# A deformable convolution and a mixture of experts on one core: the weight tables of the next image, with ten tent buffers across both halves of the partitions

## The chip, the cores and the metric

The kernel runs on one NeuronCore of a Trainium2 chip. The metric is the device time of one execution in microseconds (us); smaller is better. The core has five engines that each work through their own instructions in order: TensorE (PE, with its weight loads as PEld), VectorE (DVE), ScalarE (ACT), GpSimd (POOL) and SyncE (SP). SP, ACT and POOL also issue DMA transfers, each on its own queue.

## What is computed

The input is x, 8 images of 128 channels and 64 x 64 pixels, in f32. Two layers follow each other, each on a group-normalised input and with a residual:

```python
x = x + relu(batchnorm(deform_conv(gn(x))))       # layer 0
x = x + moe_conv(gn(x))                           # layer 1

# deform_conv, k = 3, for each image
om   = conv3x3(x, off_w) + off_b                  # 27 planes: 9 x (dy, dx), 9 masks
mask = sigmoid(om[:, 18:])
py, px = pixel + tap - 1 + (dy, dx)               # real-valued positions
val  = bilinear(x, py, px) * mask                 # zero outside the image
out  = einsum('bckhw,ock->bohw', val, w)
```

Layer 1 mixes four expert convolutions by a gate on the image's mean and adds a shared one. Batch normalisation needs the statistics of all 8 images, so layer 1 starts when layer 0 is over.

## The kernel before

`dense()` computes layer 0 without gathers. An offset smaller than 2 reaches 5 rows and 5 columns around each tap, so bilinear interpolation is a sum over these with weights max(0, 1 - |distance|), a "tent" in y and one in x. Tents are made for each of `NR = 5` distances. The y tents are multiplied by the mask.

**Bands.** An image is `NB = 8` bands of 8 rows. For a band, `pick` (L606) copies overlapping 8 x 8 pixel patches on DVE, `pixels` transposes them on PE (L621) and ACT copies them out of PSUM (L626) into `xt`. `weights` (L648, DVE) multiplies an x weight tile (`xwts`, three buffers) and a y weight tile (`ywts`, two buffers) to a matrix `s`. `sample` multiplies `xt` by `s` on PE (L664), ACT copies the result to `samples` (L674), and DVE copies an edge column of the first and last of the five groups (L686, L688). `conv` runs the nine taps of the deformable convolution on PE (L716); ACT adds the bias (L724), DVE takes statistics (L725), and SP stores the band (L726, `yd`).

**Tables.** The weight tiles come from two tables in DRAM for each image, `taby` and `tabx` (two copies, in turn). `load_x` (L592) and `load_y` (L577) bring a band's part in, issued on POOL two bands ahead: 2 loads of 576 KB and 8 of 90 KB. The generator `tables(b)` makes an image's tables while the image before is worked on:

- SP loads the image into `pads`; DVE takes statistics (L267); two small matmuls (L273, L283) and POOL (L289) give the group normalisation; ACT and DVE apply it (L295, L296).
- `combine` (L322, DVE) forms half sums of rows in two buffers, `combos`, and `tap` (L339, PE) runs the offset convolution on them; ACT and DVE collect it in `om` (L361, L368 to L383). ACT copies part of it with rows and columns exchanged (L388).
- SP stores it to DRAM as `rowwise` (L394) and `colwise` (L398) and loads it back spread over 64 partitions (L416, `spread`, 15 loads), as `off_y`, `mask` and `off_x` side by side on partitions 0 to 63 of `combos[1]`. DVE mends the edges (L441 to L444) and ACT takes the sigmoid of the mask (L448).
- For each of five distances: ACT makes the x tent (L505 the distance, L511 the tent), DVE the y tent (L516, L518) and its product with the mask (L524). SP stores both to the tables: `store_x` (L495, five or six transfers of up to 34 KB) and `store_y` (L468).

For images 1 to 7 the tents have two buffers of each kind, all on partitions 0 to 63:

```python
work = a1.tile([W, 2, 2, YSTEP], F32, name="work", tag="om")
tents = [[work[:, a, i % 2] for i in range(NR)] for a in range(2)]
```

**Order.** The schedule is by hand (`manual_schedule`): each engine runs its instructions in program order. The generator yields between its pieces (`pause`), and the band loop calls `next(made)` a fixed number of times: once after each of five sample groups, and once or twice after each convolution tap:

```python
for _ in range(1 if calls > TAPS else 1 + (done % 3 > 0)):
    next(made, None)
```

At band 6 of an image, what is left of the generator is run at once, and that for the image after the next starts.

**Head.** For image 0 the tables are made with nothing beside them. `FIRST = 3` bands' x tents are made and stored first (`early_x`), x stores alternating between POOL and SP, y stores on SP; then come the loads of bands 0 and 1, the x tents of the other columns, and their 28 stores on SP. `tabx` is laid out by patch row q, then row tile, then column: `QROW = NROW * XROW`.

`layer1()` follows; the change doesn't touch it.

Of the kernel before, what the change touches and what calls it, by code (L numbers as in the profile page):

```python
# [55 lines left out]
GROW = NR * YSTEP  # L56
XROW = (NCOL + 1) * T * XSTEP
QROW = NROW * XROW
# [5 lines left out]
def deform_moe_conv(  # L64
# [83 lines left out]
    def padded(pool, name):  # L148
# [12 lines left out]
        for a, n in (("y", (H + 2 * REACH) * GROW), ("x", Q * QROW))  # L161
# [15 lines left out]
    def dense():  # L177

        with ExitStack() as st:
# [32 lines left out]
            for i, at in ((0, 0), (1, H - 1)):  # L212
                nc.gpsimd.affine_select(
                    out=nudge[:, i : i + 1], in_=nudge[:, i : i + 1], compare_op=ALU.is_equal,
                    fill=0.0, base=-at, pattern=[[0, 1]], channel_multiplier=1,
                )

            combos = [a1.tile([P, H // 2, W], F32, name=f"combo{i}") for i in range(2)]
            flat = combos[1].rearrange("p h w -> p (h w)")
            three = flat[0:W, 0 : 3 * ROW].rearrange("p (t v k) -> p t v k", t=3, v=3)  # L220
            off_y, mask, off_x = (
                flat[0:W, i * ROW : (i + 1) * ROW].rearrange("p (v u j) -> p v u j", u=3, v=3)
                for i in range(3)
            )
            every_u = flat[0:W, 0 : 3 * ROW].rearrange("p (a u j) -> p a u j", u=3, j=WB)
            tent_y = combos[0].rearrange("p h w -> p (h w)")[0:W, 0:YSTEP]
# [16 lines left out]
            def tables(b):  # L243
# [8 lines left out]
                beside = nc.sync if b else nc.gpsimd  # L252
# [18 lines left out]
                yield from pause(3)  # L271
                pm = ps_c.tile([P, CH], F32, name="pm", tag="pc")
                nc.tensor.matmul(pm[:, 0:1], lhsT=gsel, rhs=mv[:, 0:1], start=True, stop=True)  # L273
                yield from pause(3)
# [6 lines left out]
                yield from pause(2)  # L281
                pv = ps_c.tile([P, CH], F32, name="pv", tag="pc")
                nc.tensor.matmul(pv[:, 0:1], lhsT=gsel, rhs=ev, start=True, stop=True)  # L283
                yield from pause(3)
                ve = small.tile([P, 1], F32, name="ve")
                nc.vector.tensor_scalar(ve, pv[:, 0:1], GN_EPS, None, ALU.add)
                yield from pause(2)
                scale = small.tile([P, 1], F32, name="scale")
                nc.gpsimd.tensor_tensor(scale, ve, nhalf, ALU.pow)  # L289
                yield from pause(3)  # L290
# [3 lines left out]
                for c in range(0, NCH, 2):  # L294
# [4 lines left out]
                    yield  # L299
# [10 lines left out]
                def combine(j):  # L310
# [5 lines left out]
                    for half in range(2):  # L316
# [5 lines left out]
                        nc.vector.tensor_tensor(  # L322
                            combo_of[j][:, half * n : half * n + n], *rows, op
                        )
                        yield
# [67 lines left out]
                for j in range(4):  # L393
# [4 lines left out]
                    beside.dma_start(  # L398
# [6 lines left out]
                if b == 0:  # L405
                    for g in range(2):
                        pick(g)
                    for _ in pixels(0):
                        pass
                yield from pause(9)  # L410
# [15 lines left out]
                for k in range(3):  # L426
# [6 lines left out]
                    for outs, parts, v in places:  # L433
                        for t, c in ((off_y, 3 * k), (mask, 2 * TAPS + 3 * k)):
                            spread(t, parts, v, nc.sync, by_row[outs, c : c + 3])
                        spread(
                            off_x, parts, v, nc.sync if b else nc.scalar,
                            colwise[b][k::3].rearrange("s w h -> w s h")[outs],
                        )
                yield from pause(14)  # L440
                nc.vector.tensor_copy(every_u[:, :, 0, 1:2], every_u[:, :, 2, 0:1])  # L441
                nc.vector.tensor_copy(every_u[:, :, 2, W : W + 1], every_u[:, :, 0, W + 1 : WB])
                for i in range(2):
                    nc.vector.tensor_scalar(  # L444
                        three[:, 0::2, 2 * i], three[:, 0::2, 2 * i], nudge[0:W, i : i + 1],
                        None, ALU.add,
                    )
                nc.scalar.activation(mask, mask, AF.Sigmoid)  # L448

                if b:  # L450
                    work = a1.tile([W, 2, 2, YSTEP], F32, name="work", tag="om")
                    tents = [[work[:, a, i % 2] for i in range(NR)] for a in range(2)]
                else:
                    one = samples[0].rearrange("p m x w -> p (m x w)")[0:W]
                    tents = [[one[:, i * YSTEP : (i + 1) * YSTEP] for i in range(NR)]]
                    one = combos[0].rearrange("p h w -> p (h w)")[0:W, YSTEP:]
                    n = FIRST * 2 * XSTEP
                    early_x = [one[:, i * n : (i + 1) * n] for i in range(NR)]
                    late = [om.rearrange("p a n -> p (a n)")[0:W], one[:, NR * n :]]
                    n = YSTEP - n  # L460
                    late_x = [late[i // 4][:, i % 4 * n : (i % 4 + 1) * n] for i in range(NR)]
# [922 lines left out]
```

## Time and profile before

| | us |
|---|---|
| median of 3 runs | 1786.99 (1786.05 to 1791.42) |
| the profiled execution | 1793.52 |
| its span | 1791.8 |
| PE busy | 1450.2 (81%) |
| DVE busy | 932.7 (52%) |
| ACT busy | 718.2 (40%) |
| POOL busy | 496.6 (28%) |
| first sample matmul (L664) starts | 89.33 |
| first band handed to ACT (L724) | 136.1 |
| last band handed to ACT | 1406.6 |

The span lies within the execution; 1.7 us are around it. The first 89 us are the head, then bands run to 1407, then layer 1. A share of busy time is an average over these: from 1461 on, in layer 1, PE is busy 322.4 of 330.8 us; from 127.7 to 1402 it is 1064.6 of 1274.3. "Granted clock" is the share of full speed that PE's clock had in a stretch. A wait names the instruction that was idle and what ended it; it costs time only where the idle engine holds up the one that sets the pace.

### The profile page before, as it was taken

Reading aid. Unit: us, or ns where it says so; the run is one execution under the profiler, and the core shown is the slowest. Engines: PE = TensorE matmul, PEld = TensorE weight load, DVE = VectorE, ACT = ScalarE, POOL = GpSimd, SP = SyncE. Lnnn points to the kernel's source line nnn. Section 1 sums busy time; section 2 is a strip of 40 time slices with the busy share of each in tenths; the row PEclk is TensorE's granted clock in tenths of the full one; section 3 lists DMA queues with packets and bytes.
Section 4 is the critical chain, followed back from the end, with each engine's and each line's share of the span. In section 5 each row is a group of like instructions: output and inputs, shape, how many; then the busy total and the mean of one; then the engine's idle time right before and its main releaser. Section 6 shows DMA issues by size and latency. Waiting matters only on the chain. (4 is left out here: it accounts for less than half of the span.)

```text
span 1791.8 us, 21276 instructions
## 1 busy us (share of the span) xinstructions
PE 1450.2 (81%) x7714; PEld 793.3 (44%) x7714; DVE 932.7 (52%) x1892; ACT 718.2 (40%) x984; POOL 496.6 (28%) x777
## 2 busy tenths in 40 slices
PE   4059758959986996899489869976999479999998
PEld 1045435426543653465255436543655234444443
DVE  5336435344633554364345345543333488888882
ACT  2224443445444543444354445344444323333330
POOL 2323123213321422232132224222332322232210
PEclk8569978979987998799789979987999789999999
DMA  5445456538454745555475547464664523334311
GB/s 184 109 96 134 102 132 147 129 78 202 105 129 109 192 109 129 138 144 135 86 179 127 125 100 193 119 140 94 167 168 113 198 92 141 141 150 152 132 48 61
DMA packets 169024, 234.31 MB, mean 131 GB/s; under 512 B 120026, under 2 KB 123384, under 8 KB 160460
## 3 DMA queue, kind: packets, MB, share of 16 engines
q0 software_dynamic: 59680, 122.86, 29.3%
q1 hardware_dynamic: 108432, 109.46, 20.4%
q8 instruction: 63, 1.03, 0.3%
q10 hardware_dynamic: 796, 0.52, 0.1%
q14 instruction: 53, 0.43, 0.1%
HBM read 180.23 MB, written 52.32 MB: 130 GB/s over the span
## 5 line engine op out<-in xcount | busy, mean ns | idle before, releaser
L716 PE MATMUL py<-samples,dw_sb 128*128 128x512 f32 (+3 forms) x1296 | 630.6, 600 | 101.0 <-ACT y L724 101.0
L577 POOL DMA_DIRECT2D ywts<-taby x508 | 303.9, 619 | 774.9 <-DVE s L648 706.4
L664 PE MATMUL pq<-s,xt 64*128 64x144 f32 (+1 forms) x3840 | 318.9, 309 | 60.8 <-DVE s L648 47.3
L674 ACT COPY samples<-pq 128x864 f32<-128x864 f32 (+1 forms) x320 | 296.7, 961 | 176.9 <-PE pq L664 176.8
L716 PEld LDWEIGHTS py<-samples,dw_sb 128*128 128x128 f32 x1296 | 225.4, 199 | 265.9 <-issue 127.9
L664 PEld LDWEIGHTS pq<-s,xt 64*128 64x128 f32 x3840 | 265.1, 192 | 171.0 <-issue 66.7
L626 ACT COPY xt<-pt 128x512 f32<-128x512 f32 (+1 forms) x256 | 142.8, 558 | 265.8 <-PE pt L621 264.8
L648 DVE TENSOR_TENSOR s<-xwts,ywts 128x432 f32<-128x432 f32 (+1 forms) x448 | 205.4, 495 | 84.3 <-PE pq L664 33.0
L621 PE MATMUL pt<-ident,picked 128*128 128x128 f32 x960 | 158.3, 287 | 96.9 <-ACT xt L626 92.9
L621 PEld LDWEIGHTS pt<-ident,picked 128*128 128x128 f32 x960 | 127.0, 148 | 236.5 <-issue 124.5
L1298 PE MATMUL pc<-v,u 128*128 128x512 f32 x384 | 172.8, 599 | 9.3 <-DVE u L1247 9.3
L1298 PE MATMUL pc<-v,wmix 128*128 128x512 f32 x384 | 176.3, 604 | 0.0
L688 DVE COPY samples<-pq 128x24 f32<-128x24 f32 x64 | 12.9, 201 | 278.5 <-ACT samples L674 278.5
L725 DVE BATCH_NORM_STATS2 ystats<-y 128x6 f32<-128x512 f32 (+3 forms) x72 | 45.7, 635 | 201.9 <-ACT y L724 201.9
L1298 PEld LDWEIGHTS pc<-v,u 128*128 128x128 f32 x384 | 72.4, 190 | 98.3 <-issue 85.8
L1298 PEld LDWEIGHTS pc<-v,wmix 128*128 128x128 f32 x384 | 72.6, 192 | 88.9 <-issue 85.2
L505 ACT ACTIVATE work<-combo,steps 64x576 f32<-64x576 f32 x35 | 46.3, 1323 | 146.6 <-DMA tabx<-work 120.3
L592 POOL DMA_DIRECT2D xwts<-tabx x128 | 75.1, 603 | 101.1 <-DMA tabx<-work 45.0
L1276 ACT ACTIVATE t<-pc,bmix 128x512 f32<-128x512 f32 x32 | 22.0, 687 | 183.1 <-PE pc L1298 101.1
L724 ACT ACTIVATE y<-py,db_sb 128x512 f32<-128x512 f32 (+3 forms) x72 | 45.7, 635 | 108.4 <-PE py L716 108.4
L322 DVE TENSOR_TENSOR combo<-pad 128x1024 f32<-128x1024 f32 x64 | 76.4, 1218 | 11.8 <-PE pc L339 9.9
L606 DVE COPY picked<-pad 128x960 f32<-128x960 f32 x128 | 82.2, 684 | 0.0
(153 smaller groups left out, 1040.5 us busy)
## 6 DMA issues: line engine op xcount, KB each, us to landing
xwts<-tabx POOLq DMA_DIRECT2D x128, 576.0 KB, 9.7
ywts<-taby POOLq DMA_DIRECT2D x508, 90.0 KB, 4.1
pad<-in_x_dram SPq DMA_DIRECT2D x48, 512.0 KB
out_dram<-yo SPq DMA_DIRECT2D x32, 512.0 KB
yd<-y SPq DMA_DIRECT2D x48, 256.0 KB
pad<-yd SPq DMA_DIRECT2D x16, 512.0 KB
x<-yd SPq DMA_DIRECT2D x16, 512.0 KB
xt<-in_x_dram SPq DMA_DIRECT2D x16, 512.0 KB
```

Source lines behind the costliest of these rows:

```text
L322: nc.vector.tensor_tensor(combo_of[j][:, half * n : half * n + n], *rows, op)
L505: nc.scalar.activation(one.rearrange("p (w y x) -> p x y w", y=3, x=3), by_bases[..., bases], AF.Abs, bias=steps[0:W, i : i + 1],)
L577: engine.dma_start(out=y_wts[g % 2][at : at + NR * Q, r].rearrange("p a b c -> p (a b c)"), in_=bass.AP(tensor=y_table[b].tensor, offset=y ...
L592: engine.dma_start(out=x_wts[g % 3][HALF * h : HALF * h + HALF], in_=bass.AP(tensor=x_table[b].tensor, offset=x_table[b].offset + (2 * j + ...
L606: nc.vector.tensor_copy(picked[g % 2][:, :, h], bass.AP(tensor=one.tensor, offset=one.offset, ap=[list(one.ap[0]), [T, NCOL], [W, Q], [1, Q]],
L621: nc.tensor.transpose(pt[:, c], picked[g % 2][:, c0 + c].rearrange("p h y x -> p (h y x)"), ident,)
L626: nc.scalar.copy(xts[g][:, c0 : c0 + n], pt[:, 0:n])
L648: nc.vector.tensor_tensor(s[:, :, 3 * at : 3 * (at + k)].rearrange("p m (c x) -> p m c x", x=3), by_x[:, :, c : c + k], by_y[:, :, w : w + ...
L664: nc.tensor.matmul(by_m[:, h, :, at : at + k], lhsT=xts[g][rows, c], rhs=s[rows, :, at : at + k], start=True, stop=True,)
L674: nc.scalar.copy(bass.AP(tensor=one.tensor, offset=one.offset + first, ap=[list(one.ap[0]), [M * PLANE, 2], [PLANE, M], [WB + 1, 3], [1, w ...
L716: nc.tensor.matmul(py, lhsT=dw_sb[:, 3 * (2 - yy) + 2 - xx], rhs=samples[g % 2][:, m : m + 3 * n - 2 : 3, xx, 1 : W + 1], start=(i == 0), ...
L1298: nc.tensor.matmul(pc, lhsT=us[j][:, kx], rhs=vs[g][:, rows, kx : kx + W], start=(kx == 0), stop=(kx == 2),)
```

## The change

- The tents get five buffers of each kind. The x tents, with `off_x`, `early_x` and the edge correction, move to partitions 64 to 127; the y tents and the mask stay on 0 to 63. The y distance before the product has two scratch tiles.
- For images 1 to 7, POOL makes the y product in two instructions (the maximum with 0, then the product) where DVE had three; and POOL forms the second half of each half sum.
- Of the x stores every second one goes to POOL's queue; so do the loads of `off_x` and the colwise stores of images 1 to 7.
- The band loop calls `next(made)` two or three times a tap (one or two in the double convolution at an image's end) where it did once or twice, and the pauses in the generator are longer.
- `tabx` is laid out by row tile first (`JROW`), then q.
- In the head, `EARLY = 2` bands' x tents are stored band by band, all five tents to a transfer; band 0's x loads are issued ahead of the y part; the two colwise stores of ACT, the mask's spread loads on ACT, and the late stores on SP and POOL share the queues. The transposes of band 0 come after the spread loads.

```diff
+EARLY = 2
-QROW = NROW * XROW
+JROW = Q * XROW
...
             flat = combos[1].rearrange("p h w -> p (h w)")
-            three = flat[0:W, 0 : 3 * ROW].rearrange("p (t v k) -> p t v k", t=3, v=3)
+            two_sides = flat[:, 0 : 2 * ROW].rearrange("p (t v k) -> p t v k", t=2, v=3)
             off_y, mask, off_x = (
-                flat[0:W, i * ROW : (i + 1) * ROW].rearrange("p (v u j) -> p v u j", u=3, v=3)
-                for i in range(3)
+                flat[sides, i * ROW : (i + 1) * ROW].rearrange("p (v u j) -> p v u j", u=3, v=3)
+                for sides, i in ((slice(0, W), 0), (slice(0, W), 1), (slice(W, P), 0))
             )
-            tent_y = combos[0].rearrange("p h w -> p (h w)")[0:W, 0:YSTEP]
+            space = combos[0].rearrange("p h w -> p (h w)")
+            tents_y = [space[0:W, 2 * i * YSTEP : (2 * i + 1) * YSTEP] for i in range(2)]
+            last = space[:, YSTEP : 2 * YSTEP]
+            early_x = space[W:P, 2 * YSTEP : 2 * YSTEP + NR * 2 * EARLY * XSTEP].rearrange(
+                "p (i n) -> p i n", i=NR
+            )
...
-                        nc.vector.tensor_tensor(
+                        engine = nc.gpsimd if b and half else nc.vector
+                        engine.tensor_tensor(
                             combo_of[j][:, half * n : half * n + n], *rows, op
                         )
-                        yield
+                    yield from pause(3)
...
-                    beside.dma_start(
+                    (nc.gpsimd if b or j % 2 else nc.scalar).dma_start(
                         out=colwise[b][:, :, H // 4 * j : H // 4 * (j + 1)],
...
-                yield from pause(9)
+                yield from pause(12)
...
-                            spread(t, parts, v, nc.sync, by_row[outs, c : c + 3])
+                            engine = nc.sync if b or t is off_y else nc.scalar
+                            spread(t, parts, v, engine, by_row[outs, c : c + 3])
                         spread(
-                            off_x, parts, v, nc.sync if b else nc.scalar,
+                            off_x, parts, v, nc.gpsimd,
...
-                yield from pause(14)
+                yield from pause(26)
...
-                if b:
-                    work = a1.tile([W, 2, 2, YSTEP], F32, name="work", tag="om")
-                    tents = [[work[:, a, i % 2] for i in range(NR)] for a in range(2)]
+                work = a1.tile([P, NR - 1, YSTEP], F32, name="work", tag="om")
+                both = [work[:, i] for i in range(NR - 1)] + [last]
...
+                def masked(i):
+                    if b:
+                        nc.gpsimd.tensor_scalar(
+                            tents_y[i % 2], tents_y[i % 2], 0.0, None, ALU.max
+                        )
+                        nc.gpsimd.tensor_tensor(
+                            both[i][0:W].rearrange("p (v j u) -> p v u j", v=3, u=3),
+                            tents_y[i % 2].rearrange("p (v u j) -> p v u j", u=3, v=3),
+                            mask[..., 1 : W + 1], ALU.mult,
+                        )
+                        return
...
                     for i in range(NR):
-                        distance_x(i, every, tents[1][i])
+                        distance_x(i, every, both[i][W:P])
+                        yield
                         yield from distance_y(i)
-                        tent_x(tents[1][i])
-                        yield
-                        tent_y_of(i)
-                        store_x(tents[1][i], i, 0, (nc.sync,))
-                        yield
+                        yield from pause(2)
+                        tent(both[i][W:P])
+                        yield from pause(2)
+                        masked(i)
+                        store_x(i, 0, (nc.sync, nc.gpsimd))
+                        yield from pause(2)
                         store_y(i)
                         yield
...
                 for i in range(NR):
-                    distance_x(i, early, early_x[i])
-                    tent_x(early_x[i])
+                    distance_x(i, first, early_x[:, i])
+                    tent(early_x[:, i])
+                store_early(0, (nc.gpsimd, nc.sync))
+                load_x(0, nc.gpsimd)
                 for i in range(NR):
                     for _ in distance_y(i):
                         pass
-                    tent_y_of(i)
-                    store_x(early_x[i], i, 0, (nc.gpsimd, nc.sync))
+                    masked(i)
                     store_y(i)
-                load_x(0, nc.gpsimd)
-                for i in range(2):
+                store_early(2, (nc.gpsimd, nc.sync))
+                late_x = [both[i][W:P, 2 * EARLY * XSTEP :] for i in range(NR)]
+                for i in range(NR):
                     distance_x(i, rest, late_x[i])
-                    tent_x(late_x[i])
+                    tent(late_x[i])
                 for k in range(2 * T):
-                    load_y(0, k, nc.gpsimd if k % 2 else nc.scalar)
-                for i in range(2, NR):
-                    distance_x(i, rest, late_x[i])
-                    tent_x(late_x[i])
+                    load_y(0, k, nc.gpsimd if k % 2 else nc.sync)
                 load_x(1, nc.gpsimd)
                 for k in range(2 * T):
                     load_y(1, k, nc.gpsimd)
                 for i in range(NR):
-                    store_x(late_x[i], i, 2 * FIRST, (nc.sync,))
+                    store_x(i, 2 * EARLY, (nc.sync, nc.gpsimd))
...
-                        for _ in range(1 if calls > TAPS else 1 + (done % 3 > 0)):
+                        for _ in range((2 if calls <= TAPS else 1) + (done % 2 or g < NB)):
                             next(made, None)
```

`store_early(j0, engines)` is new: for the row tiles j0 and j0 + 1 (one band) it issues eight transfers each, four of 15 columns x 5 tents and four for the edge columns. Each run in DRAM is 144 bytes, as before.

## The prediction

> **What bounds the kernel now.** I read the windows first, cut at the times at which the deformable convolution hands a band to ScalarE (L724), then the waits, then the order in time of one bad stretch. Columns of the windows: stretch, its length, busy time of PE, PEld, DVE, ACT and POOL (instructions), granted PE clock, DMA share, GB/s.
>
> ```profile
> 985.68:1004.25 18.57, 18.57 (x127) 9.61 (x129) 8.11 (x17) 9.24 (x11) 6.10 (x10) 1.00 0.50 123
> 1004.25:1028.19 23.94, 16.36 (x117) 10.16 (x117) 7.36 (x18) 9.22 (x13) 6.05 (x10) 0.93 0.62 129
> 1028.19:1064.99 36.80, 19.77 (x93) 10.93 (x93) 16.45 (x37) 15.12 (x20) 5.62 (x10) 0.78 0.43 92
> 1080.41:1095.12 14.71, 14.71 (x95) 8.73 (x97) 5.62 (x13) 7.51 (x11) 5.95 (x10) 1.00 0.85 232
> 1324.18:1338.84 14.66, 14.66 (x95) 8.67 (x97) 5.62 (x13) 7.52 (x11) 6.05 (x10) 1.00 0.77 186
> ```
>
> A plain band is PE and nothing else: 14.66 us, PE busy throughout at full clock. Two bands of every image are not: 23.94 and 36.80 us, at clock 0.93 and 0.78. The other images show the same pair (24.2 and 36.9, 24.5 and 37.0, 24.0 and 37.1, 26.0 and 37.2, 23.9 and 36.8 us). Image 1 has one of 47.9 us instead.
>
> ```profile
> POOL ywts L577 <- DVE s L648: 706.4, 50, 31.0
> ACT work L505 <- DMA tabx<-work: 120.3, 24, 8.3
> ACT combo L448 <- DVE combo L444: 64.0, 8, 11.0
> DVE combo L441 <- DMA combo<-colwise: 63.3, 7, 10.5
> DVE work L524 <- DMA taby<-work: 55.4, 15, 7.0
> PE pq L664 <- DVE s L648: 47.3, 1, 47.3
> DVE s L648 <- DMA xwts<-tabx: 22.4, 5, 16.0
> ```
>
> (Total us, times, longest.) ScalarE waits 120 us to overwrite a tent buffer that a store is still reading; VectorE 55 us for the y buffers; and once an image for the spread offsets (L441), ScalarE behind it (L448). How that reaches PE, in order of time (start, length; in brackets the idle time before and its releaser):
>
> ```profile
> 871.23 1.35 ACT L505 ACTIVATE work<-combo,steps 64x576 f32<-64x576 f32 x1 [4.53 <-DMA tabx<-work]
> 873.32 4.60 SPq L495 DMA_DIRECT2D tabx<-work  x6
> 882.88 1.34 ACT L505 ACTIVATE work<-combo,steps 64x576 f32<-64x576 f32 x1 [8.31 <-DMA tabx<-work]
> 886.06 0.90 PE L621 MATMUL pt<-ident,picked 128*128 128x128 f32 x3 [8.58 <-ACT xt L626]
> 863.14 2.08 PE L716 MATMUL py<-samples,dw_sb 128*128 128x512 f32 x2 [10.36 <-ACT y L724]
> ```
>
> Tent 1's x part is ready at 873.3; SP issues its six stores until 877.9; the last lands so that ScalarE may write tent 3 into that buffer at 882.88. ScalarE works in order: the copy of PE's transposes is queued behind tent 3, and PE stands still for 8.58 us. The 10.36 us at 863.14 come the same way from L441. The head (image 0) has its own two:
>
> ```profile
> 89.33 6.72 PE L664 MATMUL pq<-s,xt 64*128 64x216 f32 x60 [47.30 <-DVE s L648]
> 127.69 0.59 PE L273 MATMUL pm<-mv,gsel 128*128 128x1 f32 x2 [16.40 <-DVE mv L270]
> 75.11 30.01 SPq L495 DMA_DIRECT2D tabx<-om  x23
> ```
>
> The first is the load of band 0's weights, the second band 2's x weights (VectorE waits 16.0 us for xwts, in order), which wait for 28 late stores that SP issues alone, 1.3 us each, until 109.
>
> **The Trainium skill.** "SBUF — State Buffer", Who interferes with whom: a VectorE instruction with two SBUF inputs and a GpSimd one that reads SBUF exclude each other for the whole instruction. The trace allows it: POOL's 128x512 addition (L1126) takes 1.26 us at least, 1.45 in the mean and 2.29 at most beside a busy VectorE. "TensorE: Matmul & The Clock Gate", Part 1: an idle PE falls to half clock and needs about 3.4 us of work to come back; here the clock is 0.50 in 860 to 867, after the stall. "Trainium Kernel Development and Optimization", Key Constraints: queues of several engines share the same DMA engines, so a second one saves issue time only. Agrees: in 850 to 855 the DMA share is 1.04 with the spreads in flight.
>
> **Part by part.** The sum is against the profiled run (1793.5 us, span 1791.8); it lies 6.5 us above the median of 1787.0, which I take off at the end.
>
> *Floor of an image.* From the windows: six plain bands of 14.66, one of 13.66, the last band's 10.54 and 6.43 us, makes 118.6. The offset convolution adds 12 taps, 1.91 us a pair (L339): 11.5. Small matmuls 0.4. Together 130.5. Images 2 to 7 now take 993.7 us between 299.8 and 1293.5, 165.6 each: 35.1 above the floor.
>
> *Five buffers (L505, L524), stores on two queues.* Tent i no longer waits for the store of tent i-2 within an image: both reuse waits (120 and 55 us) go. SP issues three of each tent's five or six x stores, POOL the rest. What is late next: ScalarE itself. A tent costs it 1.32 + 0.68 us, five 10.0, in a stretch of about 1.4 bands (20 us) in which its own band work is 7.5 per 14.66, so 10.2: it is just full. PE has about 1 us of slack at each copy; I charge 4.5 us an image (bounds 1 and 9).
>
> *Wider steps.* Counting the steps that a band hands out (now 5 + 15, then 5 + 23 to 27) and the pauses: stores to spread loads 12 steps, on to L441 26 more, about 20 us. Needed: POOL's four colwise stores 4 x 0.92 (L398 in the head), landing 4.6, five loads of about 0.65, landing about 4, so 16. In the kernel before SP issued all 15 loads itself and waited 6.4 us among them. The 10 us wait should go; 0.5 us charged (bounds 0 and 8). The five tents spread over 1.4 bands instead of one. Image 1 still empties its last two tents at once: 3 us. Normalisation and its small matmuls, with longer pauses: 1.5 us (now 3 to 4).
>
> *VectorE work moved to POOL.* An image sends POOL four half sums (128x1024), five max and product pairs (64x576), 13 x stores, 4 colwise stores, 5 loads. Prices: POOL's 128x528 additions in layer 1 (L1214) took 1.10 us, so 64x576 1.2 to 2.6, taken 1.6; one-input 0.9, between 0.5 at the rate of a memset (L231, 2304 elements in 2.02) and 1.2; half sums 2.3 (2.1 to 4.6); x store 0.67, between 0.56 (90 runs, L495) and 0.92 (576 runs, L398). A tent: 2.5 + 1.7 = 4.2 us. The image: 21 + 9.2 + 3.7 + 3.2 = 37 us, beside 80 load issues of 0.61, 49. POOL goes to 86 of 140 us. In the tents' 20 us it has 21 + 8.6 to do and falls some 10 us behind. Queued behind it are the ywts and xwts loads of the band after next. Cover: POOL waits 12 to 14 us a band for s (the 706 us), and the loads have a band until VectorE, another 10 us until PE. Charge 1 us (bounds 0 and 15), 1 more for PE taps waiting for a half sum. Without the cover each late load shows in full.
>
> Charges: 4.5 + 0.5 + 1.5 + 1 + 1, and 0.5 for ScalarE's 1.9 us turn copy, are 9 us. Images 2 to 7: (35.1 - 9) x 6 = 157.
>
> *Image 1* (136.1 to 299.8, 163.7 us): its eight pieces have a floor of 116.5; with 11 us charged, 36 gained.
>
> *Head, x table by row tiles, stores by band.* x loads of band 0 start when its own 16 stores are out, before the y part. Early tents end near 51 (now 53.3), stores out at 56, landed 58, x loads to about 66 beside the y tents (VectorE needs 12.9 us from 46, as now); y stores landed 61; 8 band-1 x stores on each queue to 63.5; y loads of band 0 issued to 66, landed 70. s at 70 instead of 88.5: 18 us. Then 15 late stores on each of two queues, done near 85, band 2's x loads landed near 94, wanted near 98: the second stall (16.4) goes, and about 3 us of half clock. 37 at most; 4 kept for the crowded DMA: 33.
>
> Sum: 157 + 36 + 33 = 226; 1793.5 - 226 = 1567.5; in terms of the median 1561. Layer 1 (1402 on) is not touched.
>
> **Rivals.**
> 1. *POOL is the new bound.* For: it takes the slow half of the sums, its queue carries the loads, and the lock can double an instruction. Against: 61% busy, 12 to 14 us of slack a band. 15 us more an image: 1561 + 105 = 1666.
> 2. *The spread loads stay late.* For: DMA share 1.04 there, some 1,700 runs of 256 bytes an image as before. Against: the window of 20 us, POOL and SP issuing together. 8 us x 7: 1617.
> 3. *Slower.* POOL's product and the loads queued behind it lock step: VectorE's distance i waits for the product i-2 (two y scratch tiles), s waits for the loads, the loads wait for s. It decides once a tent takes POOL over about 11 us instead of 4.2, the price of the gain: 226 us over 35 tents is 6.5. At 12 us: about 1805. Against: no POOL row with 576 elements costs above 2.6 by scale.
> 4. *The waits stay* (a buffer still shared): 1785. Against: in the instruction order the five tents write four slices of work and one of combo, and distances run ahead of products.
>
> **Numbers.** Forecast 0.63, rivals 0.16, 0.14, 0.06, 0.01. The forecast's own range is 1515 (charges of 3 us, head 37) to 1610; with rival 2 and the near part of rival 1 it reaches 1645, leaving about 2 in 10 out. What a measurement can tell from no change is about 0.3%, some 5 us. Faster 0.93, within 0.01, slower 0.06.
>
> **What would show it.** Right: no wait of L505's successor on tabx stores nor of the y product on taby; no band above about 19 us after image 1; first sample matmul near 71 us; PE clock near 1.0 between 150 and the end of layer 0; layer 0 over near 1180. Wrong if POOL is busy throughout and s waits for ywts; if the DVE edge copies still wait 10 us for colwise; if ScalarE is full in the tents' bands and PE waits for its copies by more than 5 us an image; or if the head's first sample stays past 80.

## The result and the profile after

The change brought the median from 1788.2 to 1731.0 us (four runs each), a ratio of 0.968, with a 95% interval of 0.965 to 0.971. The profiled execution took 1730.8 us, its span 1729.1. That is 57 us gained where 226 were forecast, and 1731 lies outside the range of 1515 to 1645. The sign was right and the size was not.

Between the first and the last band that the deformable convolution hands to ScalarE (L781 now) lie 1223.3 us (121.8 to 1345.1) instead of 1270.5. So 47 us were gained in the images, where 193 were forecast, and 14 in the head, where 33 were. The expert layer after it is as long as before (385.2 and 384.0 us).

Line numbers have moved. In the kernel after, ScalarE's distance and tent are L551 and L557, GpSimd's max and product L571 and L574, the x stores L489, the y and x weight loads L634 and L649, VectorE's sample weights L705; the kernels of the experiments have theirs a few lines off.

First the waits of the kernel after (engine and instruction that wait, what ended the wait; total us, times, longest):

```profile
POOL ywts L634 <- DMA xwts<-tabx: 164.0, 55, 6.7
ACT work L551 <- DMA tabx<-work: 152.1, 21, 13.7
POOL ywts L634 <- DVE s L705: 106.5, 25, 10.9
```

ScalarE's wait before a tent, the one that the change was forecast to remove, is still there and longer: 152 us instead of 120. It comes 21 times, three times in each of seven images. The wait for a y buffer (55 us before) is gone. And GpSimd no longer waits 706 us for VectorE to free a weight tile, only 106; in their place it waits 164 us for its own earlier loads to land. The wait for the spread offsets (10 us an image before) is gone: the edge copies (L452) wait 9.5 us for it once, in the head, and not again.

Then the windows of one image, cut as in the prediction (stretch, length, busy time of PE, PEld, DVE, ACT, POOL, clock, DMA share, GB/s):

```profile
791.44:824.17 32.73, 17.44 (x117) 10.89 (x117) 9.78 (x22) 13.35 (x17) 19.68 (x28) 0.78 0.52 111
824.17:845.04 20.87, 17.37 (x71) 9.12 (x73) 9.59 (x18) 11.91 (x16) 17.48 (x19) 0.77 0.53 126
...
874.39:894.81 20.42, 16.88 (x99) 9.89 (x101) 10.76 (x26) 8.32 (x12) 8.41 (x14) 0.92 0.89 197
```

The bad pair of bands (23.9 and 36.8 us before) is now 32.7 and 20.9, 53.6 us instead of 60.7. The clock still falls to 0.78, and GpSimd is busy for 60% and 84% of the two. The third line is a band of 14.7 to 14.9 before; the next image's input and statistics fall into it. The wider steps alone do not explain its growth: with the old pace put back (below) it still has 18 to 23 us.

How one tent holds up the next, from the timelines of the four engines, put in order of time:

```profile
801.18 0.68 ACT L557 ACTIVATE work<-work 64x576 f32<-64x576 f32 x1
801.88 2.24 SPq L489 DMA_DIRECT2D tabx<-work  x3
806.77 0.56 POOL L634 DMA_DIRECT2D ywts<-taby  x1 [1.41 <-DMA xwts<-tabx]
807.36 1.68 POOL L571 TENSOR_SCALAR combo<-combo 64x576 f32<-64x576 f32 x1
809.12 1.31 POOL L574 TENSOR_TENSOR work<-combo,combo 64x576 f32<-64x576 f32 x1
810.38 1.29 POOL L489 DMA_DIRECT2D tabx<-work  x2
813.46 1.31 ACT L551 ACTIVATE work<-combo,steps 64x576 f32<-64x576 f32 x1 [10.99 <-DMA tabx<-work]
816.12 1.81 PE L721 MATMUL pq<-s,xt 64*128 64x144 f32 x12 [9.05 <-DVE samples L745]
```

The first tent's x part is ready at 801.9. SyncE issues its three stores at once. GpSimd's two come only at 810.4, because they stand behind weight loads that wait for earlier loads and behind the max and the product (L571, L574). ScalarE wants to write the second tent, into a slice that no tent of this image has used yet, and waits 10.99 us until those two stores have landed. PE stands still for 9.05 us. The third tent waits for the second in the same way (5.88 us) and the fourth for the third (4.83). The fifth does not wait.

The head, with lines of PE, ScalarE and GpSimd:

```profile
66.03 0.57 POOL L649 DMA_DIRECT2D xwts<-tabx  x1 [7.87 <-DMA tabx<-combo]
74.34 2.32 POOL L634 DMA_DIRECT2D ywts<-taby  x4 [0.24 <-DMA tabx<-combo]
75.15 1.06 ACT L551 ACTIVATE combo<-combo,steps 64x432 f32<-64x432 f32 x1 [16.73 <-DMA tabx<-combo]
80.40 7.37 PE L721 MATMUL pq<-s,xt 64*128 64x216 f32 x60 [33.31 <-DVE s L705]
114.96 0.59 PE L291 MATMUL pv<-e,gsel 128*128 128x1 f32 x2 [11.26 <-DVE e L286]
```

The first sample comes at 80.4 (forecast 71, before 89.3), just past the 80 that the prediction named as a sign of being wrong; the second stall shrank from 16.4 to 11.3 us.

### The profile page after: what moved, and what is told of

Its sections match the earlier page's. It is cut to its first block, busy times and chain, and to the rows that moved or that the text cites. A ratio compares the mean times of both kernels' runs of the same rounds, so it can differ in the third digit from the quotient of the medians.

```text
span 1729.1 us, 21429 instructions
## 1 busy us (share of the span) xinstructions
PE 1443.5 (83%) x7714; PEld 793.2 (46%) x7714; DVE 941.5 (54%) x1759; ACT 725.2 (42%) x984; POOL 801.9 (46%) x1048
## 3 DMA queue, kind: packets, MB, share of 16 engines
q8 instruction: 63, 1.03, 0.3%
## 4 chain that ended last, share of the span: by engine, by line
PE 53%; DMA 19%; POOL 9%; DVE 5%; ACT 5%; issue 3%; SPq 0%; POOLq 0%; ACTq 0%; DVEq 0%
PE pc L1354 18%; PE py L773 17%; PE pq L721 9%; DMA xwts<-tabx 6%; DMA pad<-in_x_dram 5%; PE pc L348 5%; DMA tabx<-work 4%; PE pt L678 3%; POOL combo L571 2%; POOL work L574 2%; POOL ywts L634 2%; ACT work L551 2%; DMA ywts<-taby 1%; ACT samples L731 1%; POOL tabx L489 1%
## 5 line engine op out<-in xcount | busy, mean ns | idle before, releaser
L773 PE MATMUL py<-samples,dw_sb 128*128 128x512 f32 (+3 forms) x1296 | 621.8, 594 | 57.1 <-ACT y L781 57.1
L634 POOL DMA_DIRECT2D ywts<-taby x508 | 294.1, 602 | 283.3 <-DMA xwts<-tabx 164.0
L705 DVE TENSOR_TENSOR s<-xwts,ywts 128x432 f32<-128x432 f32 (+1 forms) x448 | 240.1, 574 | 78.3 <-DMA xwts<-tabx 32.9
L678 PE MATMUL pt<-ident,picked 128*128 128x128 f32 x960 | 154.2, 282 | 23.7 <-ACT xt L683 19.7
L331 POOL TENSOR_TENSOR combo<-pad 128x1024 f32<-128x1024 f32 x28 | 80.4, 2872 | 58.9 <-ACT pad L303 49.0
L551 ACT ACTIVATE work<-combo,steps 64x576 f32<-64x576 f32 (+1 forms) x32 | 41.0, 1281 | 152.3 <-DMA tabx<-work 152.1
L663 DVE COPY picked<-pad 128x960 f32<-128x960 f32 x128 | 97.0, 799 | 0.0
L571 POOL TENSOR_SCALAR combo<-combo 64x576 f32<-64x576 f32 x35 | 60.7, 1735 | 69.2 <-DVE combo L565 68.8
L649 POOL DMA_DIRECT2D xwts<-tabx x128 | 75.6, 602 | 32.9 <-DMA ywts<-taby 16.4
```

What stands on the lines that cost most here:

```text
L331: engine.tensor_tensor(combo_of[j][:, half * n : half * n + n], *rows, op)
L571: nc.gpsimd.tensor_scalar(tents_y[i % 2], tents_y[i % 2], 0.0, None, ALU.max)
L634: engine.dma_start(out=y_wts[g % 2][at : at + NR * Q, r].rearrange("p a b c -> p (a b c)"), in_=bass.AP(tensor=y_table[b].tensor, offset=y ...
L663: nc.vector.tensor_copy(picked[g % 2][:, :, h], bass.AP(tensor=one.tensor, offset=one.offset, ap=[list(one.ap[0]), [T, NCOL], [W, Q], [1, Q]],
L678: nc.tensor.transpose(pt[:, c], picked[g % 2][:, c0 + c].rearrange("p h y x -> p (h y x)"), ident,)
L705: nc.vector.tensor_tensor(s[:, :, 3 * at : 3 * (at + k)].rearrange("p m (c x) -> p m c x", x=3), by_x[:, :, c : c + k], by_y[:, :, w : w + ...
```

## The experiments

Fifteen kernels were run. Each ratio is to the kernel before, run beside it on the same chip (its medians lay between 1787.5 and 1792.9 us); each has four runs or more. "Band n" below is the n-th stretch between hand-overs, counted from an image's first.

**Tiles or buffers.** In the trace each instruction has the semaphores that it waits for (counters; a transfer raises one when it lands). By these, tents 1 to 3 of an image (counted from 0) each wait for four transfers: the x stores of the tent just before that take every fourth partition. Tent 4, which lies in another tile, waits for none. So theory A: such a store counts as a reader of the whole tile, and four slices of one tile are one buffer. The tests were to give the tents tiles of their own, in the new kernel and in the old.

```diff
-                om = a1.tile([P, 2, HW // 4], F32, name="om", tag="om")
-                omr = om[:, 0]
+                omr = a1.tile([P, HW // 4], F32, name="omr", tag="oma")[:, :]
+                omc = a1.tile([P, HW // 4], F32, name="omc", tag="omb").rearrange(
...
-                work = a1.tile([P, NR - 1, YSTEP], F32, name="work", tag="om")
-                both = [work[:, i] for i in range(NR - 1)] + [last]
+                work_a = a1.tile([P, 2, YSTEP], F32, name="work_a", tag="oma")
+                work_b = a1.tile([P, YSTEP], F32, name="work_b", tag="omb")
+                spare = flat[:, 2 * ROW : 2 * ROW + YSTEP]
+                both = [work_a[:, 0], work_b[:, :], last, spare, work_a[:, 1]]
```

> Changed kernel with the tents of an image laid in four tiles (the two halves of the offset buffer's place, combo0, combo1) so that no tent shares a tile with the one before it; nothing else differs. Theory A (a store that takes every fourth partition counts as a reader of its whole tile, so slices of one tile give one buffer): the 21 waits of ScalarE's distance on x-table stores (152 us) fall to nearly nothing, the two bands that hold the tents (33.2 and 20.5 us) come to 14 to 20 each, 12 to 22 us an image over six images: 1600 to 1660 us. Theory B (the tents are paced by GpSimd's product and by SyncE's one queue, and the wait only shows it): the waits go but the bands stay, over 1710 us.

Measured: 1654.6 us, ratio 0.926 (0.922 to 0.929). No wait of a distance on an x store is left in images 1 to 7 (only the head's one, 19.7 us). Band 2, which had 33 to 35 us in images 2 to 7, is 15.8 to 17.0. Theory A holds. The time is at the upper end of what it gave, because a later band grew.

> Kernel before, its two tent buffers of each kind in two tiles instead of slices of one; as many buffers, one queue, nothing else. Theory A (the tile is what is waited for): tent i waits for the store of tent i-2 only, the 120 us of waits on x-table stores fall below 50, and 5 to 15 us an image go: 1690 to 1755 us. The reading that the prediction rests on (the wait is for the buffer of two tents back): nothing changes, within 0.5% of 1787 us, the wait stays near 120 us.

The edit in the kernel before, where the buffers alternate between two slices (not shown: the offset buffer `om` is split as above, and the head's late tents lie in its two halves):

```diff
-                    work = a1.tile([W, 2, 2, YSTEP], F32, name="work", tag="om")
-                    tents = [[work[:, a, i % 2] for i in range(NR)] for a in range(2)]
+                    works = [
+                        a1.tile([W, 2, YSTEP], F32, name=f"work{t}", tag=t)
+                        for t in ("oma", "omb")
+                    ]
+                    tents = [[works[i % 2][:, a] for i in range(NR)] for a in range(2)]
```

Measured: 1710.5 us, 0.958 (0.954 to 0.961). With as many buffers as before and one queue, this edit alone beats the whole change. The prediction's reading, that a tent waits for the one two back, would have left the time as it was; it falls. The waits of the distances on x stores:

```profile
ACT workomb L508 <- DMA tabx<-workoma: 40.1, 5, 8.3
ACT workomb L508 <- DMA tabx<-workomb: 11.2, 2, 8.0
ACT workoma L508 <- DMA tabx<-workoma: 9.9, 5, 3.4
```

61 us are left of 120; under 50 was expected. What is left is the wait that the prediction had in mind, for the buffer of two tents back, though the first row names the other tile. Its longest waits are those of tent 3, as here (SyncE's stores of tent 1, then ScalarE's distance of tent 3):

```profile
665.17 5.97 SPq L498 DMA_DIRECT2D tabx<-workomb  x6
678.20 1.35 ACT L508 ACTIVATE workomb<-combo,steps 64x576 f32<-64x576 f32 x1 [7.85 <-DMA tabx<-workoma]
```

The six semaphores that the second line waits for are those of the six transfers of the first, the last of them up at 678.12. The store named in the bracket, tent 2's, was issued later on one of the same semaphores.

**The work given to GpSimd.** Masked product and half sums back on VectorE, all else as changed:

```diff
-                        engine = nc.gpsimd if b and half else nc.vector
+                        engine = nc.vector
...
-                    if b:
-                        nc.gpsimd.tensor_scalar(
...
-                        return
```

> Changed kernel with the second half sums and the masked product of images 1 to 7 back on VectorE (three instructions a tent as before); nothing else. Theory A: the product is about as long, the store starts at the same time, and the wait for the tile's store still paces the tents: within 1% of 1731 us. Theory C (GpSimd as the new bound or by its pressure on VectorE): faster than 1715 us.

Measured: 1681.1 us, 0.942 (0.938 to 0.945): 50 us faster, so theory A alone was not enough. ScalarE's wait on x stores is still 108.8 us. Both causes act on one chain: the tile makes the next tent wait for all stores, and the product makes GpSimd's stores late.

> Tents in tiles of their own, and the masked product and second half sums of images 1 to 7 on VectorE: the edits of the two earlier runs together. If the two costs are separate (the tile's wait 76 us, the product on GpSimd 50 us): 1600 to 1615 us. If the loads of the weights are late in the run with own tiles because GpSimd issues them behind its products, the band before the normalisation (27 to 34 us there) falls under 18 as well: 1585 to 1605 us. If that band is long because the four loads of the next image's input come at once, it stays above 24 and the time is 1620 to 1645 us.

Both edits together: 1571.4 us, 0.877 (0.875 to 0.880). That is more than the 76 and the 50 us added (1605), and better than any case expected. First and last hand-over are 1060.2 us apart (124.4 to 1184.6). One image:

```profile
709.91:725.71 15.80, 15.80 (x111) 9.81 (x113) 11.37 (x28) 13.26 (x17) 9.18 (x16) 1.00 0.79 169
725.71:739.41 13.70, 13.56 (x81) 7.50 (x79) 11.71 (x28) 12.03 (x16) 9.09 (x15) 1.00 0.87 198
...
754.00:768.70 14.70, 14.70 (x96) 8.72 (x96) 4.46 (x11) 7.50 (x10) 5.61 (x10) 1.00 1.03 246
768.70:789.60 20.90, 18.03 (x111) 10.79 (x113) 12.93 (x31) 8.41 (x11) 8.22 (x15) 0.92 0.94 183
```

The tents' two bands (the first two lines) are nearly PE and nothing else, at full clock. ScalarE is busy for 13.3 of 15.8 us in the first and still in time.

> Tents in tiles of their own, and of the work that the change gave to GpSimd only the masked product back on VectorE; the half sums stay on GpSimd. Theory: what hurts is the product, which stands between two tents' stores and ahead of the weight loads on GpSimd; the half sums (2.9 us each, 81 us in all) lie beside other work: within 10 us of the run with both back on VectorE. Rival: the half sums cost their length on the path as well: 20 to 40 us slower than that run.

Only the product on VectorE, the half sums on GpSimd: 1576.3 us, 0.881 (0.879 to 0.882), not to be told from the run with both back. The product is what costs, 78 us once the tiles are apart (1654.6 to 1576.3); the half sums, 82 us of GpSimd's time, are hidden.

**How the product costs 78 us.** With own tiles and the product on GpSimd, the time from first to last hand-over is 86 us longer than with the product on VectorE. Some 53 of these lie in band 6 (27 to 34 us in images 1 to 6) and 25 in band 3 (18 to 21 us in images 3 to 7). The chain of waits that leads into one band 6 (start, length, what):

```profile
499.67 2.20 POOL combo L574
...
501.95 1.31 POOL work_a L577
...
504.50 1.21 POOL xwts L652 x2
505.71 12.99 DMA ywts<-taby
...
518.99 8.16 DMA xwts<-tabx
527.16 1.27 DVE s L708 x3
```

The weight loads are issued behind the products, and the last of them lands at 527.15, when VectorE has waited 20.83 us for it; PE has stood for 10.17. From 495 to 505 GpSimd is busy for 9.8 of 10 us, its DMA issues counted in, and the DMA engines have a share of 0.27; from 505 to 530 they have 1.02, and the two loads of the chain take 13.0 and 8.2 us. Band 3 shows the same want of transfers while GpSimd works:

```profile
770.43:788.33 17.90, 15.41 (x81) 8.50 (x77) 11.49 (x17) 12.14 (x15) 16.83 (x16) 0.90 0.53 122
```

GpSimd is busy for 16.8 of 17.9 us, and the DMA share is 0.53; it is 0.87 in the same band with the product on VectorE (second line of the windows above).

Four ways in which the price could come about were tried. First, the loads of the next image's input might crowd them out:

```diff
-                    yield from pause(5)
+                    yield from pause(9 if b > 1 else 5)
```

> Tents in tiles of their own, product on GpSimd as changed, and for images 2 to 7 nine steps instead of five between the four loads of an image's input. If their coming at once delays the weight loads of that band: the band of 27 to 34 us falls to 15 to 22, 7 to 12 us an image over five images, 1595 to 1620 us. If GpSimd's order delays them: within 10 us of 1655.

Measured: 1651.3 us, 0.922 (0.920 to 0.923), band 6 still 26 to 32 us. The spacing of the input loads is not it. Second, VectorE waits for GpSimd's product before it may write the third y distance (56.8 us in all with own tiles), and all sample weights behind it wait too. A third scratch buffer takes most of that away:

```diff
+                scratch = [tents_y[0], tents_y[1], work_b[0:W, 1]]
...
-                    by_dy = tents_y[i % 2].rearrange("p (k j) -> p k j", j=W)
+                    by_dy = scratch[i % 3].rearrange("p (k j) -> p k j", j=W)
```

> The run with own tiles and the product on GpSimd, with three scratch buffers instead of two between VectorE's y distance and GpSimd's product, so that VectorE waits for the product of three tents back. If the product costs its 78 us because VectorE, with all the sample weights behind it, waits for a GpSimd that itself waits for loads (the lock step of the prediction's slower rival): half or more of the waits for a third and fourth tent go, 20 to 45 us faster than 1655. If it costs because stores and loads stand behind the product on GpSimd: within 10 us of 1655.

Measured: 1676.1 us, 0.938 (0.934 to 0.941). VectorE's wait for the product fell from 56.8 to 14.6 us, bands 2 to 4 are clean (15.8, 13.7, 14.7), and bands 5 and 6 grew to 18 to 22 and 29 to 34 us. Neither theory expected 21 us slower. VectorE's lock step with GpSimd is not the price. Without it the tents come faster than GpSimd's queue can take them, it seems; that was not tried by itself. Third, the x weight loads on another queue:

```diff
-                                load_x(g + 2, nc.gpsimd)
+                                load_x(g + 2, nc.sync)
```

> Own tiles, product and half sums on GpSimd as changed (1655 us), and the two x weight loads of each band issued by SyncE instead of GpSimd. If the product costs its 78 us by holding the weight loads back in GpSimd's queue: VectorE's waits for x weights (114 us) fall below 50 and the time to 1600 to 1635 us. If it costs by GpSimd slowing VectorE, or by late x stores: within 12 us of 1655.

> Own tiles, product and half sums on VectorE (1571 us), and the two x weight loads of each band issued by SyncE. With the product gone GpSimd's queue has room, so little should move: within 12 us of 1571. If the loads still come late from GpSimd's queue in the 20 us band of the next image's input: that band falls to 15 to 17 us, 1540 to 1555 us.

Measured: 1797.9 us, 1.006 (1.004 to 1.008), with the product on GpSimd, and 1704.9 us, 0.954 (0.951 to 0.957), with it on VectorE. Both are slower than the same kernel with the loads on GpSimd, by 143 and 134 us, so the pair says nothing on the product. SyncE's own waits in the first of them show why:

```profile
SPq L786 <- ACT y L784: 440.9, 42, 29.2
```

SyncE stands in order before each store of the convolution's output, up to 29 us, with the loads behind it. Fourth, the doubled cost: the true product on VectorE, and besides an idle max and product of the same shapes on GpSimd, for which nobody waits (and one clearing of its buffer an image, not shown):

```diff
+                    if b:
+                        nc.gpsimd.tensor_scalar(idle, idle, 0.0, None, ALU.max)
+                        nc.gpsimd.tensor_tensor(
+                            idle.rearrange("p (v j u) -> p v u j", v=3, u=3),
+                            idle.rearrange("p (v j u) -> p v u j", v=3, u=3),
+                            mask[..., 1 : W + 1], ALU.mult,
+                        )
```

> Own tiles, the true product on VectorE and half sums on GpSimd (1576 us), and besides a max and a product of the same shapes on GpSimd at the same place in the order, on a scratch slice that nothing reads; the output does not depend on it. If the product on GpSimd costs by the time it takes in GpSimd's queue, ahead of the weight loads and x stores: most of the 78 us comes back, 1620 to 1665 us. If it costs because stores and VectorE wait for its result: within 15 us of 1576.

Measured: 1642.7 us, 0.917 (0.914 to 0.921): 66 of the 78 us are back. VectorE's waits for loads with the idle product, then without it:

```profile
DVE s L708 <- DMA ywts<-taby: 124.3, 13, 20.3
DVE s L708 <- DMA xwts<-tabx: 99.8, 15, 22.9
```

```profile
DVE s L698 <- DMA ywts<-taby: 71.8, 12, 20.1
DVE s L698 <- DMA xwts<-tabx: 26.8, 8, 11.0
```

So most of the price needs no wait for the product's result: its time on GpSimd, 3.6 us a tent (1.84 and 1.80) in the queue that issues the weight loads and stores, is enough. It is not lost in the same places, though: band 3 is back at 13.7 to 14.3 us, and in images 3 to 7 bands 4 to 6 have grown. How much of it is GpSimd's pressure on VectorE, an idle product can't tell. VectorE was busy for 1008.9 us instead of 954.7 with as many instructions, 16 us of these in its weight products (0.59 us instead of 0.555 in the mean, 448 times), and in band 3 of the fifth image for 13.67 of 13.70 us. Against it speaks that the half sums on GpSimd raise VectorE's busy time too (927.1 to 954.7, though they take 28 instructions from it), at no cost that can be told.

**The other parts of the change.** The old pace (pauses and steps as before) in the changed kernel, and then with own tiles and the product on VectorE:

```diff
-                        for _ in range((2 if calls <= TAPS else 1) + (done % 2 or g < NB)):
+                        for _ in range(1 if calls > TAPS else 1 + (done % 3 > 0)):
...
-                yield from pause(26)
+                yield from pause(14)
```

> Changed kernel with the old pace alone: the pauses, the steps for each matmul and the steps inside a tent as they were before; buffers, queues, tables and engines as changed. As the prediction had it (the wider steps take the wait for the spread rows, some 9 us an image, and cost nothing): 60 to 80 us slower than 1731. If their gain is mostly given back in the band of the next image's input (20.3 us instead of 14.7): within 25 us of 1731.

> Own tiles and product on VectorE, with the old pace (pauses, steps for a matmul, steps inside a tent) of the kernel before. In the changed kernel the old pace cost only 8 us. If it cost so little because the tile's waits ate what the wider steps gave: 30 to 60 us slower than 1571 here, the spread wait of some 10 us back in each image. If the wider steps give nothing in themselves: within 12 us of 1571.

Measured: 1738.8 us, 0.970 (0.965 to 0.974), against 0.968 as changed, no difference that can be told; and 1619.0 us, 0.904 (0.901 to 0.908), against 0.877, 48 us slower. The wider steps are worth 48 us, and in the changed kernel none of it was seen.

The x stores on SyncE's queue alone, with own tiles and the product on VectorE:

```diff
-                        store_x(i, 0, (nc.sync, nc.gpsimd))
+                        store_x(i, 0, (nc.sync,))
```

> Own tiles and product on VectorE, with the x stores of images 1 to 7 on SyncE's queue alone, as before the change. Theory: once no tent shares a tile with the last, the store has a band's time to land and the second queue is worth little: within 12 us of 1571. If the second queue is what lets the stores keep up: 25 us or more slower.

Measured: 1593.3 us, 0.890 (0.888 to 0.893). The second queue is worth 22 us, between the two cases. The Trainium skill says, in "Perfetto Trace Analysis", DMA Optimizations, that balancing transfers over engines may help where the issuing is what binds. Here it helped by these 22 us, less than what a product in the same queue costs; that it is the issuing that binds was not shown by itself.

**What is left.** Two runs went for the band of the next input, still 20 to 24 us:

```diff
-                    yield from pause(5)
-                yield from pause(3)
+                    yield from pause(7 if b > 1 else 5)
+                yield from pause(11 if b > 1 else 3)
```

> Own tiles and product on VectorE (1571 us), and for images 2 to 7 seven steps instead of five between the input loads and eleven instead of three before the statistics. The band of the input (19.7 to 24.3 us) has TensorE waiting 3 to 5 us for the group means: if that wait comes from statistics that are asked for before the input has landed, the band falls to 15 to 17 us, 4 to 6 us in each of five images: 1540 to 1555 us. If the loads themselves press on the weight loads, under 8 us gained.

> Own tiles, product and half sums on VectorE (1571 us), and the stores of the convolution's output issued by ScalarE, which makes it, instead of SyncE, which stands 11 to 22 us at such a store before it comes to the input loads. If the 20 us band of the input is long because those loads are issued late and all at once: it falls to 15 to 17 us and the time to 1540 to 1555. If the issues cost ScalarE more than they free: slower than 1580.

The first gave nothing: 1574.9 us, 0.880 (0.877 to 0.883). The second, one line that lets ScalarE issue the output stores, gave 1559.8 us, 0.872 (0.869 to 0.874), the fastest kernel of the study, 12 us below 1571 by the medians, though the two intervals touch. But the band did not shrink as expected: it is 15.4 us in one image and 21 to 22 in four. What holds it is open. In the windows above the DMA share is 1.03 in the band ahead of it and 0.94 in it, so the DMA engines may be full with the loads of both; that was not tried. Nor was the number of buffers, the new table layout or any part of the head tried by itself.

## Why the prediction was wrong, step by step

*Five buffers, stores on two queues: the step that failed.* The prediction read the distance at 882.88 as tent 3 waiting to write "into that buffer" of tent 1, and concluded that "both reuse waits (120 and 55 us) go". The rows of the kernel before have five distances in that image: 861.35, 871.23, 882.88, 890.61 and 897.75. The one at 882.88 is the third, tent 2, and it waited for the store of tent 1 just before it, in the other slice. Four of the five waited; if each reused the buffer of two tents back, at most three could, 21 in seven images, where the row of 120.3 us that the prediction showed counts 24. The releaser's name, tabx<-work, is the same for all slices. Had the tents been counted, the tile would have been the suspect. In the new kernel four of five tents share a tile, so three waits an image stay. The rival for this ("the waits stay", a buffer still shared) was named and got 0.01, on the ground that tents write four slices: that is the very point that was wrong. The edit of the tile is worth 76 us with the product on GpSimd and 110 us (1681.1 to 1571.4) without it.

*Work to POOL: the size was near, the cover was not.* Max and product were taken at 2.5 us and took 1.74 and 1.77 in the mean, 3.5; half sums 2.3, took 2.87; an x store 0.67, took 0.63. A tent is 5.1 us instead of 4.2. What failed is "Charge 1 us", resting on the cover: GpSimd waits 12 to 14 us a band for s. That wait was not idle room: with the product in GpSimd's order the loads are issued late, VectorE waits 222 us for them in all (99 with the product on VectorE, own tiles in both), and 1 us an image was 78 us in all, 11 an image. GpSimd's own wait for its earlier loads, 164 us in place of 48, is no mark of the product; it is 202 us with own tiles and the product on VectorE. Rival 1, "POOL is the new bound", priced it at 105 us and 1666 us; the run that leaves only this fault took 1654.6. Its chance of 0.16 was too low. Rival 3, the lock step through the scratch tiles, was tried with the third scratch and falls. Its time does not follow from its own price either: 12 us a tent instead of 4.2, 35 times, would be 273 us more than 1561, so 1834 and not 1805.

*Wider steps.* The spread wait went as forecast and rival 2 falls. The band with the normalisation, charged 1.5 us, grew by 5.7 (20.4 instead of 14.7); how much of that is the normalisation is not shown. The pace is worth 48 us as soon as the tents do not wait, some 7 an image, where the step counted on a wait of 10.

*The charge of 9 us an image, the floor of 130.5.* With both faults away four images took 134.5 to 136.1 us from first hand-over to first hand-over, 4 to 6 above the floor. The tents' charge (4.5) was not needed: ScalarE is nearly full, as forecast, but PE is busy for 29.36 of the 29.5 us of their two bands. What lies above the floor is in band 6. The images gain 210 us there, where 193 were forecast.

*Head.* 33 forecast, 14 measured. The second x load of band 0 waited 7.87 us for a table store, the y loads were issued from 70.2 on SyncE and 74.3 on GpSimd instead of by 66 because the stores of band 1 came first, and the fifth late tent waited 16.73 us for early stores from combo, its own tile: the same fault once more. The working missed these orders. This was read from the trace and not tried.

With own tiles and the work given to GpSimd back on VectorE the kernel takes 1571 us, against a forecast of 1561: two faults, one of reading and one of cover, stand between it and 1731. That the sum comes so near is in part luck. This kernel lacks the work on GpSimd that the forecast counted in, and of the terms the images gained 17 us more and the head about 20 less than forecast.

## What to carry to other kernels

Before a wait is put down to the reuse of a buffer, count the instances and see which transfer each one waits for: the name in the trace is the tile's, and can be that of a later transfer on the same semaphore, and slices of a tile are buffers only if the program's waits tell them apart. Time that an engine spends waiting is no cover if the same engine issues the transfers that others wait for; put idle work there and measure what it costs. And an edit that shows nothing may be worth much behind a wait that hides it: the pace gave nothing in the changed kernel and 48 us in the mended one.

## What was not expected of the hardware

GpSimd's one-input max of 64x576 took 1.64 us at least and 1.74 in the mean, longer than its two-input product of as many elements (1.31 at least), and start to start in the timeline it is 1.76. VectorE's one-input instruction of that shape takes 0.74. The Trainium skill, "GPSIMD Engine Reference", Engine selection, has one-input work roughly at line rate and two-input work about twice as slow as on VectorE. The first does not hold here: 2.4 times VectorE's time. The second does: a half sum of 128x1024 takes GpSimd 2.34 us at least, VectorE 1.22.

GpSimd's half sums took 4.93 us at most. VectorE's 1.22 us half took 4.57 us once, from 911.10 to 915.67, around GpSimd's from 912.16 to 914.58, and 1.74 us in the mean of 36, where it was 1.22 in the kernel before. That agrees with the exclusion that the prediction cited, and in that one case the two halves side by side took longer than VectorE's two in turn (2.35 to 2.49 us).
